# Linear attention and a mixture of experts on one core: the rarely needed blocks spread their outputs by 0/1 matmuls and SP transfers

## The chip, the cores and the metric

The kernel runs on one core of a Trainium2 chip. A core has TensorE (PE: matmuls; PEld in the profile is its weight load), VectorE (DVE), ScalarE (ACT), GpSimd (POOL), and SyncE (SP, which here only issues transfers). Each has its own instruction queue, and they wait for one another by semaphores. Transfers are made by 16 DMA engines; this kernel issues them from SP's, ACT's and Pool's queues. The metric is the device time of one execution in microseconds (us), as the median of several runs.

## The reference

The input x has 4 batches of 512 tokens with 256 features. Two layers follow, each added to its own input:

```python
x = x + attention(layernorm(x), ...)          # linear attention, 16 heads of 16
x = x + ffn(layernorm(x), gate, w0, w1, wo)   # mixture of 8 experts, the best 2 for each token
# ffn:
gate_logits = x @ gate                        # 8 per token
top_k_weights = softmax(the two largest)
out = sum over the two experts e:  weight * ((silu(x @ w0[e]) * (x @ w1[e])) @ wo[e])
```

The expert weights are 256 x 512 (w0, w1) and 512 x 256 (wo). So 2048 tokens with two experts each give 4096 rows of expert work, and how many go to which expert depends on the data.

## The kernel before, in words

**Stages.** The attention of each batch runs as a generator of 15 steps; batch b begins 4 steps after batch b - 1. Each batch writes its new x to the DRAM tile `y` (L386, on ACT's queue) and then, for each of its tokens and both chosen experts, sends a row (256 features, weight, token number) to a region of the DRAM tile `xg` that belongs to the expert: eight indirect transfers per batch on Pool's queue (L469), 32 in all.

**Blocks.** The expert work goes by blocks of 128 rows of one expert. For each block, `fetch` loads the rows from `xg` (SP's queue), `turn` transposes them and copies the expert's w0 and w1 into a staging area, `half` (L618) and `hidden` make silu(h0) * h1, and `finish` (L631 to L656) multiplies by the third weights (L640), scales each row by its weight (L645) and scatter-adds the 128 rows to their tokens by an indirect transfer on Pool's queue (L649). `advance` keeps four blocks in flight, one in each of these steps.

**How many blocks.** It isn't known when the program is built how many full blocks there are. FULL = 32 is the most there can be, USUAL = 28, SURE = 25 and EARLY = 9. Nine blocks ("early") start before the last batches are through; eight more ("last") are the part-filled ends of the experts' regions. Of the others ("full"), 16 are always there, three more usually, and those from `USUAL - EARLY` = 19 on are called `rare`: four blocks. `plan` makes a table of rows and experts; a block that doesn't exist is pointed at spare rows and does its work on those. The number of full blocks found is written to `found` (L564).

**Where results go.** The early and last blocks and the first three full ones are added to `y`. Ahead of the first block of `held` one transfer on Pool's queue copies `y` to the output (L648); the 16 held blocks are then added to the output itself (`whole`).

**The end.** At L710 every engine reads `found`, and at L711 a runtime branch (`tc.If`) asks if more than 19 full blocks were found. If so, the body runs: it zeroes `y` by four SP transfers, runs the rare blocks (which are scatter-added to `y` by four Pool transfers), loads `y` back batch by batch on SP's queue, and adds it to the output by four accumulating transfers on Pool's queue (L720 to L725). If not, every engine jumps to a skipping path[...]; its instructions carry the line L711. Behind both paths lies the program's end (L767): SP waits for all counts, each engine drains, and a barrier over the five engines closes the kernel.

Of the kernel before, what the change touches and what calls it, by code (L numbers as in the profile page):

```python
# [9 lines left out]
F32 = mybir.dt.float32  # L10
I32 = mybir.dt.int32
U32 = mybir.dt.uint32
AF = mybir.ActivationFunctionType
ALU = mybir.AluOpType
# [7 lines left out]
P = 128  # L22
# [9 lines left out]
def kernel(  # L32
# [29 lines left out]
    nc = tc.nc  # L62
    B, N, E = x.shape
    NE, _, M = w0.shape
    NT = N // P
# [6 lines left out]
    USUAL = FULL - NE // 2  # L72
    EARLY = 2 * N * TOPK // P - NE + 1
# [6 lines left out]
    xpool = ctx.enter_context(tc.tile_pool(name="x", bufs=B))  # L80
    carry = ctx.enter_context(tc.tile_pool(name="carry", bufs=2))
    work = ctx.enter_context(tc.tile_pool(name="work", bufs=2))
# [3 lines left out]
    psum = ctx.enter_context(tc.tile_pool(name="psum", bufs=8, space=PSUM))  # L86
# [18 lines left out]
    y = dram.tile([T + P, E], F32, name="y")  # L105
# [29 lines left out]
    for e in range(NE):  # L135
        for i, src in enumerate((w0, w1)):
            nc.sync.dma_start(
                out=hw_sb[i][:, bass.ts(e, OW)].rearrange("p (c m) -> p c m", c=EC),
                in_=src[e].rearrange("(c p) m -> p c m", p=P),
# [4 lines left out]
    def load_w2():  # L144
# [13 lines left out]
        out=head_mask, in_=head_mask, compare_op=ALU.is_ge, fill=0.0, base=0,  # L158
        pattern=[[-HEAD_DIM, HPC], [0, HEAD_DIM]], channel_multiplier=1,
    )  # L160
    nc.gpsimd.affine_select(
        out=head_mask, in_=head_mask, compare_op=ALU.is_ge, fill=0.0, base=HEAD_DIM - 1,
        pattern=[[HEAD_DIM, HPC], [0, HEAD_DIM]], channel_multiplier=-1,
# [6 lines left out]
        out=upto, in_=upto, compare_op=ALU.is_ge, fill=0.0, base=0,  # L170
        pattern=[[1, NE], [-1, NE]], channel_multiplier=0,
# [5 lines left out]
        out=earlier, in_=earlier, compare_op=ALU.is_ge, fill=0.0, base=-1,  # L177
        pattern=[[1, P]], channel_multiplier=-1,
# [4 lines left out]
    def counting(name, shape, pattern, base=0, per_partition=0, dtype=F32):  # L183
        t = const.tile(shape, dtype, name=name)
        nc.gpsimd.iota(
            t, pattern=pattern, base=base, channel_multiplier=per_partition,
            allow_small_or_imprecise_dtypes=True,
        )
        return t
# [8 lines left out]
    rows = counting("rows", [1, FULL], [[P, FULL]])  # L198
# [374 lines left out]
    def read(entry, most, *engines):  # L573

        loads, (value,) = nc.values_load_multi_w_load_instructions(  # L575
            entry, engines=list(engines), min_val=0, max_val=most,
            skip_runtime_bounds_check_because="plan() keeps it within them",
        )
        for ins in loads:
            tc.keep_in_program_order(ins)  # L580
        return value
# [49 lines left out]
    def finish(block, g, it):  # L631

        j, b, e, row, place = block
        if e is not None:
            at = e * OW
        else:
            at = read(place, (NE - 1) * OW, mybir.EngineType.PE)
        ps = psum.tile([P, E], F32, tag="a", name=f"eo_{j}")
        for m in range(MC):
            nc.tensor.matmul(  # L640
                ps, lhsT=it[:, m, :], rhs=w2_sb[:, bass.ds(at + m * E, E)],
                start=(m == 0), stop=(m == MC - 1),
            )
        ys = blk.tile([P, E], F32, tag="ys", name=f"ys_{j}")
        nc.vector.tensor_scalar(ys, ps, g[:, E : E + 1], None, ALU.mult)  # L645
        full = block in held
        if full and block is held[0]:
            nc.gpsimd.dma_start(out=whole, in_=y[0:T, :])  # L648
        ins = nc.gpsimd.indirect_dma_start(  # L649
            out=whole[:, :] if full else y[:, :], out_offset=bass.IndirectOffsetOnAxis(ap=g[:, E + 1 : E + 2].bitcast(I32), axis=0),  # L650
            in_=ys, in_offset=None, bounds_check=(T if full else T + P) - 1, oob_is_err=True, compute_op=ALU.add,
        )
        if full:
            return
        tc.declare_no_dep(ins.ins, group=f"after {b}", reason="tokens of batches up to b")
        tc.add_to_no_dep_group("adds", ins.ins)  # L656

    whole = out.rearrange("b n e -> (b n) e")
    fetched, turned, made, held = [], [], [], []

    def advance(block=None):


        if block is not None:
            fetched.append(fetch(block))
        if fetched and (len(fetched) > 1 or block is None):
            turned.append(turn(*fetched.pop(0)))
        block = turned.pop(0) if turned and (len(turned) > 1 or not fetched) else None
        if block:
            s = work.tile([P, MC, P], F32, tag="s", name=f"s_{block[0][0]}")  # L670
            nc.scalar.activation(s, half(0, *block), AF.Silu)
        if made:
            finish(*made.pop(0))
        if block:
            made.append(hidden(s, *block))


    state = {"staged": 0, "turned": 0, "count": spread}
# [5 lines left out]
    for at in range(max(begin) + STAGES + 1):  # L684
# [11 lines left out]
        if ready:  # L696
            block = ready.pop(0)
# [4 lines left out]
    pad(end)  # L702
    blocks = plan(tot, FULL - EARLY, B - 1, "full")
    held += blocks[: SURE - EARLY]
    rare = blocks[USUAL - EARLY :]
    for block in last + blocks[SURE - EARLY : USUAL - EARLY] + held:
        advance(block)
    while fetched or turned or made:
        advance()
    many = read(state["found"], FULL, *ENGINES)  # L710
    with tc.If(many > USUAL - EARLY):  # L711
        zero = xpool.tile([P, NT, E], F32, tag="x", name="zero")
        nc.gpsimd.memset(zero, 0.0)
        for b in range(B):
            nc.sync.dma_start(out=y[b * N : (b + 1) * N, :].rearrange("(t p) e -> p t e", p=P), in_=zero)
        for block in rare:
            advance(block)
        while fetched or turned or made:
            advance()
        for b in range(B):  # L720
            extra = xpool.tile([P, NT, E], F32, tag="x", name=f"extra_{b}")
            nc.sync.dma_start(out=extra, in_=y[b * N : (b + 1) * N, :].rearrange("(t p) e -> p t e", p=P))
            nc.gpsimd.dma_start(
                out=out[b].rearrange("(t p) e -> p t e", p=P), in_=extra, accum_op=ALU.add
            )  # L725


# [43 lines left out]
```

## Time and profile before

| what | value |
|---|---|
| median of the runs | 348.0 us (3 runs, 347.77 to 349.11) |
| the profiled execution's own time | 349.94 us |
| its span, first to last instruction | 348.1 us |
| mean granted TensorE clock in it | 0.949 |
| PE busy / PEld busy | 303.4 us (87%) / 266.6 us (77%) |
| DVE busy / ACT busy / POOL busy | 155.5 us / 127.3 us / 113.3 us |
| transfers | 35.59 MB in 27873 packets |
| of these on Pool's (software) queue | 6768 packets, 11.08 MB |

A row of the group table reads: line, engine, operation, output<-input, number of instructions | busy us in all, mean ns of one | idle time of the engine ahead of them in us, and what ended it. Register, branch, semaphore and drain instructions are not counted as busy; the profile lists them for a line under the engine's name with a q (POOLq is Pool's sequencer). For such a line it gives the durations (least, median, most) in ns and when the first and the last of them started, in us from the span's start.

### The profile page before, as it was taken

To read this page: it belongs to the slowest core of one execution; us is meant where nothing else is said; L and a number is where in the kernel's file an instruction comes from. 1 tells how busy PE (TensorE), PEld (TensorE's weight loads), DVE (VectorE), ACT (ScalarE), POOL (GpSimd) and SP (SyncE) were. 2 spreads that over 40 slices of the span, in tenths; PEclk is the share of its full clock that TensorE was granted. 3 is DMA by queue.
4 is the path that set the end of the run, shared out by engine and by line. 5 is a ranking of instruction groups with operands and counts; after the bars stand their busy time and mean duration, and the time that the engine had idled before them with its cause. 6 is when DMAs were issued, how large, how long until landed. Compare 5 with 4: busy or idle time off the path is not lost. (4 is left out here: it accounts for less than half of the span.)

```text
span 348.1 us, 6093 instructions
## 1 busy us (share of the span) xinstructions
PE 303.4 (87%) x2136; PEld 266.6 (77%) x2136; DVE 155.5 (45%) x525; ACT 127.3 (37%) x200; POOL 113.3 (33%) x147
## 2 busy tenths in 40 slices
PE   0999899899852898995999999999999999999930
PEld 0567686676741787995999999999999999999920
DVE  4856879785793662643312212232332323334110
ACT  1446738556333155352212111342433334243100
POOL 5510301347055075355322313233203333323230
PEclk9999999999975799998799999999999999999985
DMA  7999021072372632236423233332372334321220
GB/s 211 368 386 385 25 70 55 1 221 84 105 260 82 200 115 49 32 93 179 96 48 48 46 50 48 58 45 49 45 258 38 55 61 63 47 30 19 29 35 0
DMA packets 27873, 35.59 MB, mean 102 GB/s; under 512 B 2849, under 2 KB 22689, under 8 KB 27809
## 3 DMA queue, kind: packets, MB, share of 16 engines
q1 hardware_dynamic: 18960, 22.00, 19.8%
q0 software_dynamic: 6768, 11.08, 17.4%
q10 hardware_dynamic: 2112, 2.10, 2.0%
q8 instruction: 19, 0.31, 0.4%
q14 instruction: 14, 0.11, 0.1%
HBM read 22.89 MB, written 14.37 MB: 107 GB/s over the span
## 5 line engine op out<-in xcount | busy, mean ns | idle before, releaser
L618 PE MATMUL hp_full<-arena 128*128 128x128 f32 x608 | 73.9, 275 | 0.0
L618 PEld LDWEIGHTS hp_full<-arena 128*128 128x128 f32 x608 | 72.3, 192 | 1.0
L649 POOL DMA_INDIRECT out_dram<-ys_full,g_full x16 | 25.2, 1574 | 58.9 <-DVE ys_full L645 27.8
L618 PE MATMUL hp_early<-arena 128*128 128x128 f32 x288 | 37.7, 284 | 5.3 <-issue 3.6
L618 PEld LDWEIGHTS hp_early<-arena 128*128 128x128 f32 x288 | 36.2, 200 | 5.3 <-issue 3.0
L469 POOL DMA_INDIRECT xg<-hn,idx_i x32 | 32.3, 1009 | 24.2 <-issue 10.2
L640 PE MATMUL eo_full<-arena,it_full 128*128 x152 | 36.1, 380 | 0.9 <-DVE it_full L628 0.9
L618 PE MATMUL hp_last<-arena,w_sb 128*128 128x128 f32 x256 | 31.2, 275 | 0.0
L618 PEld LDWEIGHTS hp_last<-arena,w_sb 128*128 128x128 f32 x256 | 30.5, 192 | 0.4
L640 PEld LDWEIGHTS eo_full<-arena,it_full 128*128 128x128 f32 x152 | 27.4, 190 | 4.0 <-DVE it_full L628 1.0
L610 ACT COPY arena<-w_sb 128x1024 f32 x28 | 29.3, 1046 | 2.8 <-DVE mv L222 1.3
L645 DVE TENSOR_SCALAR ys_full<-eo_full,g_full 128x256 f32<-128x256 f32 x19 | 9.2, 483 | 45.0 <-PE eo_full L640 45.0
L602 ACT COPY arena<-gp_full 128x256 f32<-128x256 f32 x19 | 7.1, 372 | 59.6 <-PE gp_full L599 56.4
L628 DVE TENSOR_TENSOR it_full<-s_full,hp_full 128x512 f32<-128x512 f32 x19 | 13.1, 687 | 26.0 <-PE hp_full L618 26.0
L265 POOL TENSOR_TENSOR x<-x,bo 128x256 f32<-128x256 f32 x16 | 12.1, 782 | 37.7 <-DVE arena L248 30.3
L649 POOL DMA_INDIRECT y<-ys_early,g_early x9 | 14.0, 1557 | 28.1 <-DVE ys_early L645 24.6
L649 POOL DMA_INDIRECT y<-ys_last,g_last x8 | 12.4, 1548 | 31.8 <-DVE ys_last L645 31.8
L379 PE MATMUL ap<-wo,arena 128*128 128x256 f32 x64 | 17.5, 431 | 3.8 <-DVE arena L371 2.5
L610 DVE COPY arena<-w_sb 128x1024 f32 x28 | 19.6, 701 | 1.6 <-issue 1.4
L379 PEld LDWEIGHTS ap<-wo,arena 128*128 128x128 f32 x64 | 13.4, 217 | 7.0 <-DVE arena L371 3.2
L640 PE MATMUL eo_early<-arena,it_early 128*128 x72 | 18.3, 400 | 0.4 <-DVE it_early L628 0.4
L277 PE MATMUL qp<-arena,wqk 128*128 128x512 f32 x32 | 16.6, 667 | 0.2 <-ACT arena L270 0.2
(168 smaller groups left out, 442.6 us busy)
## 6 DMA issues: line engine op xcount, KB each, us to landing
w_sb<-in_w_dram SPq DMA_DIRECT2D x16, 512.0 KB
arena<-in_w_dram SPq DMA_DIRECT2D x8, 512.0 KB
g_full<-xg SPq DMA_DIRECT2D x19, 130.0 KB
x<-in_x_dram SPq DMA_DIRECT2D x4, 512.0 KB
y<-x ACTq DMA_DIRECT2D x4, 512.0 KB
xg<-empty SPq DMA_DIRECT2D x9, 130.0 KB
g_early<-xg SPq DMA_DIRECT2D x9, 130.0 KB
g_last<-xg SPq DMA_DIRECT2D x8, 130.0 KB
```

Source lines behind the costliest of these rows:

```text
L265: nc.gpsimd.tensor_tensor(xb[:, t, :], xb[:, t, :], bo_sb, ALU.add)
L277: nc.tensor.matmul(ps, lhsT=wqk_sb[:, k, bass.ts(c, P)], rhs=xT[:, k, :], start=(k == 0), stop=(k == EC - 1),)
L379: nc.tensor.matmul(ps[:, t - t0, :], lhsT=yT[:, c, bass.ts(t, P)], rhs=wo_sb[:, c, :], start=(c == 0), stop=(c == EC - 1),)
L469: apart(nc.gpsimd.indirect_dma_start(out=xg[:, :], out_offset=bass.IndirectOffsetOnAxis(ap=idx_i[:, t, k : k + 1], axis=0), in_=hn[:, t, k ...
L602: nc.scalar.copy(gT, ps)
L610: copy(w[i], hw_sb[i][:, bass.ds(at, OW)])
L618: nc.tensor.matmul(ps[:, m, :], lhsT=w[i][:, bass.ds(k * M + m * P, P)], rhs=gT[:, k, :], start=(k == 0), stop=(k == EC - 1),)
L628: nc.vector.tensor_tensor(it, s, ps, ALU.mult)
L640: nc.tensor.matmul(ps, lhsT=it[:, m, :], rhs=w2_sb[:, bass.ds(at + m * E, E)], start=(m == 0), stop=(m == MC - 1),)
L645: nc.vector.tensor_scalar(ys, ps, g[:, E : E + 1], None, ALU.mult)
L649: ins = nc.gpsimd.indirect_dma_start(out=whole[:, :] if full else y[:, :], out_offset=bass.IndirectOffsetOnAxis(ap=g[:, E + 1 : E + 2].bit ...
```

## The change

`finish` gets an early end for rare blocks: instead of the scatter-add, the scaled rows are kept in an SBUF tile (`made`), and their token numbers in a column of another (`whose`). In the body of the `tc.If`, `y` isn't used any more. A row of numbers 0 to 511 is made once by Pool's iota. For each batch, SP loads the output's rows; DVE compares the token numbers with the row of numbers, which gives a 0/1 matrix for each of the four rare blocks, and lowers the token numbers by 512 for the next batch; PE multiplies these matrices with the kept rows, four matmuls summed in PSUM for each of four tiles of 128 tokens; DVE adds the sums to the loaded rows, and SP stores them. The body has no transfer on Pool's queue any more. Ahead of the branch, the only difference is that `rare` is made as an empty list first and filled in place.

```diff
@@ finish
+        if block in rare:
+            k = rare.index(block)
+            nc.vector.tensor_scalar(state["made"][:, k, :], ps, g[:, E : E + 1], None, ALU.mult)
+            nc.vector.tensor_copy(state["whose"][:, k : k + 1], g[:, E + 1 : E + 2].bitcast(I32))
+            return
         ys = blk.tile([P, E], F32, tag="ys", name=f"ys_{j}")
...
-    fetched, turned, made, held = [], [], [], []
+    fetched, turned, made, held, rare = [], [], [], [], []
...
-    rare = blocks[USUAL - EARLY :]
+    rare += blocks[USUAL - EARLY :]
...
     with tc.If(many > USUAL - EARLY):
-        zero = xpool.tile([P, NT, E], F32, tag="x", name="zero")
-        nc.gpsimd.memset(zero, 0.0)
-        for b in range(B):
-            nc.sync.dma_start(out=y[b * N : (b + 1) * N, :].rearrange("(t p) e -> p t e", p=P), in_=zero)
+        state["made"] = xpool.tile([P, NT, E], F32, tag="x", name="rare_made")
+        lists = xpool.tile([P, NT, E], F32, tag="x", name="lists").rearrange("p t e -> p (t e)")
+        numbers, state["whose"] = lists[:, 0:N], lists[:, N : N + len(rare)]
+        nc.gpsimd.iota(
+            numbers, pattern=[[1, N]], base=0, channel_multiplier=0, allow_small_or_imprecise_dtypes=True
+        )
+        sums = [xpool.tile([P, NT, E], F32, tag="x", name=f"sums_{i}") for i in range(2)]
         for block in rare:
             advance(block)
         while fetched or turned or made:
             advance()
         for b in range(B):
-            extra = xpool.tile([P, NT, E], F32, tag="x", name=f"extra_{b}")
-            nc.sync.dma_start(out=extra, in_=y[b * N : (b + 1) * N, :].rearrange("(t p) e -> p t e", p=P))
-            nc.gpsimd.dma_start(
-                out=out[b].rearrange("(t p) e -> p t e", p=P), in_=extra, accum_op=ALU.add
-            )
+            rows = out[b].rearrange("(t p) e -> p t e", p=P)
+            nc.sync.dma_start(out=sums[b % 2], in_=rows)
+
+            at = []
+            for k in range(len(rare)):
+                at.append(work.tile([P, N], F32, tag="ex", name=f"at_{b}_{k}", bufs=4))
+                nc.vector.tensor_scalar(at[k], numbers, state["whose"][:, k : k + 1], None, ALU.is_equal)
+            nc.vector.tensor_scalar(state["whose"], state["whose"], -float(N), None, ALU.add)
+            for t in range(NT):
+                ps = psum.tile([P, E], F32, tag="a", name=f"spread_{b}_{t}")
+                for k in range(len(rare)):
+                    nc.tensor.matmul(
+                        ps, lhsT=at[k][:, bass.ts(t, P)], rhs=state["made"][:, k, :],
+                        start=(k == 0), stop=(k == len(rare) - 1),
+                    )
+                nc.vector.tensor_tensor(sums[b % 2][:, t, :], sums[b % 2][:, t, :], ps, ALU.add)
+            nc.sync.dma_start(out=rows, in_=sums[b % 2])
```

## The prediction

> **What bounds the kernel now.** I read the group table first, to see whether the edited block runs at all in this measurement.
>
> ```profile
> L618 PE MATMUL hp_full<-arena 128*128 128x128 f32 x608 | 73.9, 275 | 0.0
> ...
> L649 POOL DMA_INDIRECT out_dram<-ys_full,g_full x16 | 25.2, 1574 | 58.9 <-DVE ys_full L645 27.8
> ...
> L469 POOL DMA_INDIRECT xg<-hn,idx_i x32 | 32.3, 1009 | 24.2 <-issue 10.2
> ```
>
> A block costs two halves of 8 matmuls, each of which appears as two MATMULs: 32 per block. So `hp_full` x608 is 19 blocks, exactly USUAL - EARLY = 28 - 9. The four rare blocks would make it 23. The condition is false here, on every engine: all of the edited work (zeroing, spreading, adding) is skipped before and will be skipped after. A saving or a loss can come only from the branch, from what the skipping path does instead, and from the kernel's end behind it.
>
> So I looked at the end. First the chain of work that ended last, in order of time:
>
> ```profile
> 335.40 0.03 POOLq L575
> 335.43 1.27 POOL out_dram L649
> ```
>
> This chain ends at 336.7 us, but the span is 348.1 us: for 11.4 us (3.3% of the span) no engine does any counted work. The instructions of the `tc.If` line and of the end (L711 and L767) fill it; columns are duration min/median/max in ns, then first and last start in us:
>
> ```profile
> L711 POOLq EVENT_SEMAPHORE  x5: 17/43/43, 335.7 to 339.4; - x5
> L711 PEldq EVENT_SEMAPHORE  x2: 51/51/51, 337.0 to 337.1; - x2
> L711 PEldq COMPARE_BRANCH  x1: 3645/3645/3645, 333.3 to 333.3; - x1
> L711 DVEq COMPARE_BRANCH  x1: 72/72/72, 334.8 to 334.8; - x1
> L711 POOLq COMPARE_BRANCH  x1: 53/53/53, 335.5 to 335.5; - x1
> L711 POOLq INC_SWDGE_SEM  x1: 1564/1564/1564, 339.5 to 339.5; - x1
> ```
>
> ```profile
> L767 SPq EVENT_SEMAPHORE  x14: 17/28/28, 341.0 to 348.1; - x14
> L767 POOLq EVENT_SEMAPHORE  x4: 17/17/17, 346.9 to 348.0; - x4
> L767 POOLq DRAIN  x3: 113/188/5709, 341.1 to 347.7; - x3
> L767 SPq DRAIN  x3: 7/7/7, 341.8 to 347.1; - x3
> ```
>
> Read in time: Pool issues the last scatter-add (335.2 to 336.7). Its branch falls through to the skipping path, where five semaphore instructions run, the last at 339.4: they hold Pool until its transfers have landed, about 339.2 (in the table of stretches the DMA share is 0.49 from 338 to 339 us and 0.00 after). Then one INC_SWDGE_SEM takes 1.56 us (339.5 to 341.1). It is there because the skipped block holds transfers on Pool's queue[...]. Then Pool's DRAIN lasts 5.71 us (341.1 to 346.8). SP, which waits for the raised counts, is done at 341.8; everything else waits for Pool's drain. From 346.9 the closing barrier takes 1.3 us to the end. So the last 9 us belong to Pool alone: wait, INC_SWDGE_SEM, DRAIN, barrier.
>
> **The change part by part.**
>
> The body: 64 matmuls on PE, about 40 DVE instructions (16 comparisons, 4 subtractions, 16 additions, 4 copies) and one iota come in; one memset, four scatter-adds and four accumulating transfers on Pool's queue, four zeroing transfers and four loads on SP's queue go out, and four loads and four stores on SP's queue come in. None of it runs here: 0 us. It would cost time only if `found` exceeded 19.
>
> The last scatter-add before the branch stays (in `finish`, the early return is for rare blocks only), so its issue still ends at 336.7 and its landing still releases the waiters near 339.2.
>
> INC_SWDGE_SEM: with no Pool-queue transfer left in the body there is nothing for it to make up, so it and the four landing waits ahead of it go from Pool's path: from 336.7, Pool's last counted work, to 341.1, the drain's start, 4.4 us. Pool's other skip instruction (its own semaphore, at 335.7) stays for the iota.
>
> The DRAIN: here the trace does not say what its 5.71 us are. Two causes fit. (a) It goes through the software transfers issued before it: 32 (L469) + 36 (L649: 9 + 8 + 3 + 16) + 1 (L648) = 69, so 83 ns each. (b) It waits for something that INC_SWDGE_SEM left running. The nearest rows are Pool's other drains:
>
> ```profile
> L761 POOLq INC_SWDGE_SEM  x1: 31/31/31, 0.2 to 0.2; - x1
> ...
> L761 POOLq DRAIN  x1: 183/183/183, 0.4 to 0.4; - x1
> ```
>
> At the start an INC_SWDGE_SEM of 31 ns is followed by a drain of 183 ns, before any transfer; the two drains at the end take 113 and 188 ns. The long one is the first after 69 transfers and also the first after a long INC_SWDGE_SEM, so these rows exclude neither. I take (a): SP's wait for the raised counts is already over at 341.0, so INC_SWDGE_SEM has visibly done its work before the drain starts. And nothing else happens in the 5.7 us: the DMA share is 0.00 from 339 to 347 us[...]. Bounds of the drain in the new kernel: about 0.2 us (all of it was INC_SWDGE_SEM's) and 5.7 + 1.6 = 7.3 us (the two shared one walk, and the drain now does all).
>
> Sum for (a): drain from 336.7 for 5.7 us to 342.4, barrier 1.3 us, end at 343.7 instead of 348.1: 4.4 us less. The profiled execution took 349.94 us around that span of 348.1; the median of the runs shown is 348.0. The 1.8 us around the span do not change, so I take the 4.4 us off the median: 343.6 us.
>
> What is late next: SP's end waits. Now they run from 341.0 to 341.8, i.e. 0.8 us; then they start at the landing (339.2) and end near 340.0, hidden behind the drain by 2.4 us. If the drain were gone, they would be the path: 340.0 + 0.1 + 1.3 = 341.4.
>
> [...] INC_SWDGE_SEM at 1.56 us stands on the path, while SP's own skip instructions (nine of 12 to 72 ns) ran at 299 to 301 us, beside other work. [...] The body grows on DVE and PE and shrinks on Pool. PE is charged already and ends at 337.3, hidden. If DVE starts to stall and I charge it PE's 3.6 us, it is ready at 335.6 + 3.6 = 339.2: hidden behind Pool's drain (342.4), and by 0.8 us behind SP's 340.0 if that drain goes. [...]
>
> **The rivals.**
>
> The drain goes with INC_SWDGE_SEM (cause b). For it: the two stand next to each other, and the start's short pair fits too. Against it: the raised counts have been seen before the drain begins. Then SP's waits end it: 341.4, which is 6.7 us less than 348.1: 341.3 us.
>
> The drain's 5.7 us begin only when the last transfer has landed: 339.2 + 5.7 + 1.3 = 346.2, 1.9 us less: 346.1 us. For it: today the drain stands behind that landing anyhow, so the trace can't exclude it. Against it: the transfers before the last have long landed and could be gone through meanwhile.
>
> The change does not do what it says: an increment on the skipping path remains (some Pool transfer still counted in the block). Then 348.0. Against it: every Pool transfer in the diff's body is removed, and rare blocks return ahead of the scatter-add.
>
> Slower: INC_SWDGE_SEM does a part of the clearing that the drain then does not have to do. The place is Pool's drain, the price is its growth; the point is 346.8 - 336.7 = 10.1 us, 146 ns for each of 69 transfers instead of 83. Even with the whole 1.6 us added it is 7.3 us, ending at 345.3 and giving 345.2, still faster; so slower needs a walk nearly twice as long as anything shown.
>
> **How the numbers follow.** Likeliest, (a): 0.58, 343.6, with 342.7 if the drain overlaps the last issue (it could start at 335.8) and 345.2 with the walk's share added. Cause (b): 0.25, 341.3. Drain after landing: 0.08, 346.1. Nothing changes: 0.05. Slower: 0.04. The range 340.8 to 345.3 takes in (a) with its bounds and (b) less 0.5 us of run-to-run spread (the runs lie 347.77 to 349.11), and leaves 0.17 out. A measurement of this kernel can tell about 0.5% (1.7 us) from no change. Faster by more: 0.58 + 0.25 + 0.05 of the landing case (346.1 is just beyond 346.3) = 0.88; within: 0.03 + 0.05 = 0.08; slower: 0.04.
>
> **What would show it.** Right: `hp_full` still x608; no INC_SWDGE_SEM at the `tc.If` line; Pool's long drain of about 5.7 us starting near 336; SP's waits ending near 340; the span near 343.7. A drain under 0.3 us shows (b); a drain ending at 344.9 shows the landing case[...]. Wrong would be the whole argument if any engine works differently before 335 us: the code ahead of the branch is the same, and its times should agree to within 0.3 us.

## The result and the profile after

The changed kernel takes 343.2 us (median of 6 runs, 341.67 to 344.51) against 347.9 us of the kernel before (6 runs, 347.13 to 349.11): ratio 0.9856, 95% interval 0.9821 to 0.9891, or 4.7 us less. The forecast was 343.6 us, range 340.8 to 345.3.

The rare blocks still do not run, so no run here shows what the new body costs when it is needed. The group table of the changed kernel (`finish` has grown by five lines, so its scatter-add is L654 now) has the same counts:

```profile
L618 PE MATMUL hp_full<-arena 128*128 128x128 f32 x608 | 73.9, 275 | 0.0
...
L654 POOL DMA_INDIRECT out_dram<-ys_full,g_full x16 | 25.1, 1567 | 59.0 <-DVE ys_full L650 32.3 <-issue 12.2 <-DVE it_full L628 11.4
```

In order of time, Pool's last scatter-add in the changed kernel (start us, us):

```profile
334.10 1.54 POOL L654 DMA_INDIRECT out_dram<-ys_full,g_full  x1 [3.08 <-DVE ys_full L650]
```

Instructions of the `tc.If` line (now L716) and of the end (now L787):

```profile
L716 PEldq COMPARE_BRANCH  x1: 3365/3365/3365, 332.2 to 332.2; - x1
L716 DVEq COMPARE_BRANCH  x1: 72/72/72, 333.7 to 333.7; - x1
L716 POOLq COMPARE_BRANCH  x1: 53/53/53, 334.4 to 334.4; - x1
L716 POOLq EVENT_SEMAPHORE  x1: 17/17/17, 334.6 to 334.6; - x1
```

```profile
L787 SPq EVENT_SEMAPHORE  x14: 17/28/28, 339.1 to 342.7; - x14
L787 POOLq EVENT_SEMAPHORE  x4: 17/17/17, 342.0 to 342.7; - x4
L787 POOLq DRAIN  x3: 46/118/7249, 334.7 to 342.5; - x3
L787 SPq DRAIN  x3: 7/7/7, 339.8 to 342.2; - x3
```

INC_SWDGE_SEM is gone, and so are four of Pool's five semaphore instructions; in the trace of before the first of those four starts at 339.20, just behind the last landing (339.17). Pool comes to its drain at 334.7, while the last scatter-add is still being issued (334.1 to 335.6), and not at 341.1. The drain is still the long one: it ends at 334.71 + 7.25 = 341.96 (starts with two decimals are the trace's own), 6.3 us behind the end of the issue. SP's waits now run from 339.1 (the landing) to 339.8, beside it.

The two profiled spans differ by 5.3 us, which splits so: the last issue ends at 335.6 instead of 336.7 (1.1 us, ahead of the edited place); from there to the end of the drain it is 6.3 us instead of 10.1 (3.8 us); the closing barrier takes 0.8 us instead of 1.3 (0.5 us). The first part can't be put down to the change: with the code ahead of the branch unchanged, the last issue ends anywhere from 332.1 to 335.6 us in the profiles of the changed kernel and of E3 and E6 below. So what is worked out from the end alone is safer than the difference of two spans. Nor can the third part be put down to the change (see the barrier below).

### The profile page after: what moved, and what is told of

Read it like the earlier page. It is cut to its first block, busy times and chain, and to the rows that moved or that the text cites. A ratio compares the mean times of both kernels' runs of the same rounds, so it can differ in the third digit from the quotient of the medians.

```text
span 342.8 us, 6088 instructions
## 1 busy us (share of the span) xinstructions
PE 302.6 (88%) x2136; PEld 266.3 (78%) x2136; DVE 155.4 (45%) x525; ACT 127.1 (37%) x200; POOL 113.2 (33%) x147
## 5 line engine op out<-in xcount | busy, mean ns | idle before, releaser
L654 POOL DMA_INDIRECT out_dram<-ys_full,g_full x16 | 25.1, 1567 | 59.0 <-DVE ys_full L650 32.3
L265 POOL TENSOR_TENSOR x<-x,bo 128x256 f32<-128x256 f32 x16 | 12.1, 784 | 37.0 <-DVE arena L248 29.4
L654 POOL DMA_INDIRECT y<-ys_early,g_early x9 | 14.0, 1557 | 28.0 <-DVE ys_early L650 24.7
L654 POOL DMA_INDIRECT y<-ys_last,g_last x8 | 12.4, 1548 | 31.8 <-DVE ys_last L650 31.8
```

The source lines that it names most:

```text
L265: nc.gpsimd.tensor_tensor(xb[:, t, :], xb[:, t, :], bo_sb, ALU.add)
L654: ins = nc.gpsimd.indirect_dma_start(out=whole[:, :] if full else y[:, :], out_offset=bass.IndirectOffsetOnAxis(ap=g[:, E + 1 : E + 2].bit ...
```

## The experiments

The theory on trial (A): Pool's closing drain goes through every software transfer issued since the last drain (the "listed" ones), at 83 ns each, and what the change gained is that this walk no longer has to wait for the last landing and INC_SWDGE_SEM. Rivals: the drain has a fixed price (B); it runs for a fixed time past the last landing (C); the long drain is what INC_SWDGE_SEM leaves behind. E1 to E4 ran on one chip (kernel before there 347.1 us, 344.45 to 348.51), E5 to E8 on another (346.7 us, 345.54 to 348.43). The totals expected were counted from the 343.2 us above; the changed kernel took 341.6 us beside E6 to E8 (that is E5) and did not run beside E1 to E4. So the totals are the weak part of the expectations, and the readings of the end are the strong one.

**E1, 32 more transfers.**

```diff
+    tiny = dram.tile([32, 8], F32, name="tiny")
+    for i in range(32):
+        nc.gpsimd.dma_start(out=tiny[i : i + 1, :], in_=experts[0:1, :])
     running = [attention(b) for b in range(B)]
```

> The changed kernel with 32 more tiny transfers (32 bytes each, to a spare DRAM tile) on Pool's queue in the first 40 us, where Pool has room. 69 software transfers become 101. Theory A (Pool's closing drain goes through every software transfer issued since the last drain, 83 to 91 ns each): the drain grows by 2.7 to 2.9 us and, if the rest keeps its times, the kernel takes about 346.0 us instead of 343.2. Theory B (the drain's length is a fixed price of having used the queue) and theory C (the drain runs for a fixed time past the last landing): drain of 7.2 us as before, 343.2 us.

Measured: 351.6 us (350.51 to 352.36), ratio to the kernel before 1.0134 (1.0062 to 1.0206). The last scatter-add and the end's rows:

```profile
339.86 1.54 POOL L654 DMA_INDIRECT out_dram<-ys_full,g_full  x1 [3.09 <-DVE ys_full L650]
```

```profile
L790 SPq EVENT_SEMAPHORE  x14: 17/28/28, 343.5 to 350.5; - x14
...
L790 POOLq DRAIN  x3: 46/118/9251, 340.5 to 350.3; - x3
```

The drain ends 340.48 + 9.25 - 341.40 = 8.33 us behind the issue: 8.33 / 101 = 82.5 ns for each transfer, against 5.71 / 69 = 82.7 in the kernel before. B falls, and C too: the end is 6.2 us behind the landing (343.5), and was 2.9 in the changed kernel. The total missed the 346.0 of the expectation by 5.6 us, and the rest did not keep its times: Pool's additions of the bias to x (L265) came behind the new transfers, the first at 41.9 us instead of 12.5, and the expert work began at 129.5 instead of 121.3.

**E2, drains in between.**

```diff
+    DRAINS = (6, 12, 18, 24, 30, 35)
@@ finish, behind the scatter-add
+        state["done"] = state.get("done", 0) + 1
+        if state["done"] in DRAINS:
+            tc.keep_in_program_order(nc.gpsimd.drain())
```

> The changed kernel with a drain instruction on Pool's queue behind the 6th, 12th, 18th, 24th, 30th and 35th of the 36 scatter-adds. Theory A: each drain leaves little for the next; the first, with about 38 transfers before it, takes some 3.5 us, the others under 1 us past their last landing, and the closing drain, with one transfer before it, ends with that transfer's landing (about 339.1 in the profile). SP's waits are then the last: the end comes about 2 us earlier, 341.2 us. Theory B: the closing drain still takes its 6 to 7 us, 343.2 us or more. Theory C: it still ends 2.9 us past the last landing, 343.2 us.

Measured: 339.35 us (338.53 to 339.64), ratio 0.9789 (0.972 to 0.9857). The drains in between (L661):

```profile
L661 POOLq DRAIN  x6: 4167/4295/5911, 167.5 to 325.4; - x6
```

The 6th scatter-add, which the first of these drains follows:

```profile
167.75 1.87 POOL L655 DMA_INDIRECT y<-ys_early,g_early  x1 [3.35 <-DVE it_early L629]
```

The end:

```profile
L791 SPq EVENT_SEMAPHORE  x14: 17/28/28, 335.7 to 337.3; - x14
L791 POOLq EVENT_SEMAPHORE  x4: 17/17/17, 336.5 to 337.2; - x4
L791 POOLq DRAIN  x3: 46/118/4695, 331.1 to 337.1; - x3
```

The closing drain looks long again, 4.7 us. Read it by its end: 331.08 + 4.70 = 335.78, just behind the landing that releases SP at 335.7. It has one transfer listed and ends 0.1 us behind that landing. Now SP's waits come last, and the barrier starts at 336.5. The six drains in between cost nothing that shows: from the first to the last matmul of the full blocks' halves it is 104.6 us here, as in the changed kernel. Their 4.2 us and more are not a walk of six transfers either: each record begins 0.2 us ahead of the record of the scatter-add that it follows in the program. The five later ones end 2.4 to 2.5 us behind that issue, about when a scatter-add lands (2.1 to 2.5 us in the profiles of E1, E3 and E6). The first, with 38 transfers listed, ends at 173.4, 3.8 us behind the issue's end (169.6); 38 at 83 ns would be 3.2. The total came 1.9 us below the 341.2 expected.

**E3, one Pool transfer back in the skipped body.**

```diff
-            nc.sync.dma_start(out=rows, in_=sums[b % 2])
+            (nc.sync if b < B - 1 else nc.gpsimd).dma_start(out=rows, in_=sums[b % 2])
```

> The changed kernel with one of the four stores of the skipped body (the last batch's) on Pool's queue again, so that the skipping path has one INC_SWDGE_SEM, for one semaphore of the eight. That semaphore's last transfer before the branch is the second last scatter-add but some, so Pool does not wait for the last landing. Theory A with the prediction's account of the gain (4.4 us = wait for the last landing 2.8 + INC_SWDGE_SEM 1.6): the wait is not back, the instruction is, at up to 1.6 us, partly beside the last scatter-add's issue: 343.2 to 344.8 us. Rival (any INC_SWDGE_SEM on the path brings the whole price back): 347.9 us.

Measured: 341.8 us (340.6 to 341.98), ratio 0.9853 (0.9783 to 0.9923): 5.3 us less than the kernel before on this chip, so no loss of gain shows.

```profile
331.14 1.54 POOL L654 DMA_INDIRECT out_dram<-ys_full,g_full  x1 [3.08 <-DVE ys_full L650]
```

```profile
L716 POOLq INC_SWDGE_SEM  x1: 1544/1544/1544, 331.8 to 331.8; - x1
```

```profile
L787 POOLq DRAIN  x3: 46/113/5709, 333.4 to 339.6; - x3
```

INC_SWDGE_SEM is back, as long for the one Pool transfer in the body as for the eight before (1544 and 1564 ns). But it does not wait for the last landing here (which releases SP's waits at 335.1) and runs from 331.8 to 333.3, mostly beside the issue (331.1 to 332.7): only 0.6 us of it are exposed. The eight semaphores of the expectation are in the trace of before: the last eight scatter-adds raise eight different ones (111 to 118), and the last but one landed at 334.38, the last at 339.17. The instruction as such is not the price; its place behind the last landing is.

**E4, the kernel before with the six drains** (the edit of E2, made in the kernel before).

> The kernel before with the same six drains on Pool's queue behind scatter-adds. Theory A: the wait for the landing stays, INC_SWDGE_SEM stays (1.6 us, or less if it too goes through the transfers that are still listed), the closing drain shrinks from 5.7 us to about 0.2: 342.4 us, or 341.2 if INC_SWDGE_SEM shrinks to 0.4. The prediction's rival (the long drain belongs to INC_SWDGE_SEM): drain still 5.7 us, 347.9 us.

Measured: 339.7 us (339.17 to 340.9), ratio 0.9796 (0.9728 to 0.9864).

```profile
L715 POOLq EVENT_SEMAPHORE  x5: 17/43/43, 332.1 to 336.9; - x5
...
L715 POOLq INC_SWDGE_SEM  x1: 190/190/190, 337.3 to 337.3; - x1
```

```profile
L771 SPq EVENT_SEMAPHORE  x14: 17/28/28, 337.5 to 339.0; - x14
...
L771 POOLq DRAIN  x3: 46/112/131, 337.6 to 338.8; - x3
```

The eight transfers in the skipped body, the wait for the landing and INC_SWDGE_SEM are all there, and yet the long drain is 131 ns. So it never belonged to INC_SWDGE_SEM, which is the prediction's first rival. INC_SWDGE_SEM itself falls from 1564 to 190 ns when 1 transfer is listed and not 69: it seems to go through the list too, by an estimate from these two figures at (1564 - 190) / 68 = 20 ns each. E2 and E4 on one chip (339.35 and 339.7, overlapping runs) say what the change is worth once the list is short: nothing that can be measured. E4's total is 7.4 us below the kernel before on this chip and below both numbers expected. The end explains 5.4 us of it (from the last issue's end to the kernel's end it is 6.1 us, and was 11.4); where the other 2 us come from is not shown.

**E5, the changed kernel again**, beside E6 to E8.

> The changed kernel itself, beside the next three on one chip. Expected by every theory: about 4.7 us less than the kernel before, the closing drain about 6.3 us past the end of the last scatter-add's issue.

Measured: 341.6 us (340.48 to 343.0), ratio 0.9863 (0.9818 to 0.9908).

```profile
330.58 1.54 POOL L654 DMA_INDIRECT out_dram<-ys_full,g_full  x1 [3.09 <-DVE ys_full L650]
```

```profile
L787 SPq EVENT_SEMAPHORE  x14: 17/28/28, 335.0 to 338.6; - x14
...
L787 POOLq DRAIN  x3: 46/118/6647, 331.2 to 338.4; - x3
```

The drain ends at 331.19 + 6.65 = 337.84, 5.7 us behind the issue (332.1) and not the 6.3 expected: 69 transfers at 83 ns. The landing (335.0) is 2.8 us behind the issue; it was 3.5 in the first profile after.

**E6, Pool waits for the last landing.** `ys` of the last block is kept in `state["last_ys"]`, which the memset writes; it waited for that scatter-add's transfer (2.35 us in the second row of the profile below).

```diff
+    nc.gpsimd.memset(state["last_ys"][:, 0:1], 0.0)
     many = read(state["found"], FULL, *ENGINES)
```

> The changed kernel with one memset on Pool ahead of the branch, into the last block's output tile, so that Pool waits for the last scatter-add to land before it comes to the branch and its drain; no INC_SWDGE_SEM. Theory A in its new form (the wait for the landing is what the kernel before paid, because the drain's walk of the listed transfers can't start before it): the drain starts 2.5 to 3.4 us later, the memset and the branch's load add up to 0.9 us: 3 to 4 us more than the changed kernel, 346.0 to 347.2 us. Rival (the price was INC_SWDGE_SEM itself, 1.6 us and what it leaves to the drain): 343.2 us, or the drain shorter by what it no longer has to wait for.

Measured: 343.8 us (342.23 to 344.9), ratio 0.991 (0.9881 to 0.9939): 2.2 us more than E5.

```profile
331.56 1.54 POOL L654 DMA_INDIRECT out_dram<-ys_full,g_full  x1 [3.09 <-DVE ys_full L650]
335.46 0.10 POOL L716 MEMSET ys_full<- 128x1 f32 x1 [2.35 <-DMA out_dram<-ys_full,g_full]
```

```profile
L789 SPq EVENT_SEMAPHORE  x14: 17/28/50, 335.4 to 342.8; - x14
...
L789 POOLq DRAIN  x3: 46/113/5709, 336.3 to 342.6; - x3
```

In the profile the drain starts 336.3 - 333.1 = 3.2 us behind the issue and lasts 5709 ns, to the nanosecond what it was in the kernel before and in E3. There is no INC_SWDGE_SEM here. From the last matmul to the end it is 12.1 us, against 8.9 in E5: 3.2 us, within the 3 to 4 expected. The medians show 2.2, which is less than expected (runs of each kernel lie 2.5 to 2.7 us apart), and 343.8 is below the 346.0 expected; so it is the profile that speaks for the theory here.

**E7, two drains in between** (E2 with `DRAINS = (18, 34)`).

> The changed kernel with drains on Pool's queue behind the 18th and the 34th scatter-add only. Theory A: they take about 5 us (some 50 transfers) and 2 to 4.5 us, the closing drain ends with the last landing as with six drains: 339.4 us, 4 us less than the changed kernel. If drains work only when little has gathered, the closing drain stays long: 341 us or more.

Measured: 338.8 us (337.79 to 339.95), ratio 0.978 (0.9733 to 0.9827): 2.8 us less than E5 on the same chip, the best version found.

```profile
L661 POOLq DRAIN  x2: 4717/5408/6100, 232.2 to 320.5; - x2
```

The scatter-adds that they follow:

```profile
232.45 1.54 POOL L655 DMA_INDIRECT y<-ys_full,g_full  x1 [3.96 <-DVE ys_full L651]
```

```profile
320.74 1.54 POOL L655 DMA_INDIRECT out_dram<-ys_full,g_full  x1 [3.98 <-DVE ys_full L651]
```

The end:

```profile
L791 SPq EVENT_SEMAPHORE  x14: 17/28/28, 334.4 to 336.0; - x14
...
L791 POOLq DRAIN  x3: 46/118/3267, 331.3 to 335.8; - x3
```

The two drains end 4.3 and 2.9 us behind the issues that they follow, with 50 and 17 transfers listed. The closing drain, with two listed, ends at 331.28 + 3.27 = 334.55, with the landing (334.4). The median gain over E5 is 2.8 us and not the 4 expected: what is late next is the landing and then SP's waits of 0.8 us.

**E8, no branch.** Left out: the reading of `found`, the `tc.If` and the four rarely needed blocks, which do not run on this data.

> The changed kernel without the reading of the number found, the branch and the rarely needed blocks behind it (left out: those four blocks; they are not run on this data anyway). Theory A: the branches lie beside the last scatter-add and Pool's drain, which keeps its 6.3 us past the issue: 343.2 us, at most 0.5 less. Rival (the jump over the bigger body, PE's 3.4 us, is a part of the end): 340 us or less.

Measured: 342.3 us (340.44 to 343.13), ratio 0.9852 (0.9801 to 0.9902), against 341.6 for E5 with overlapping runs.

```profile
333.00 1.54 POOL L654 DMA_INDIRECT out_dram<-ys_full,g_full  x1 [3.08 <-DVE ys_full L650]
```

```profile
L756 POOLq DRAIN  x3: 46/113/7492, 332.8 to 340.8; - x3
```

The drain ends at 332.77 + 7.49 = 340.26, again 5.7 us behind the issue (334.5), and from the last matmul to the end it is 8.9 us in both. So PE's branch (3345 ns in E5, absent here) and the bigger body are not a part of the end.

## Why the prediction was right

**That nothing but the end could change** held in the main: the counts are the same, and the profiles differ at the `tc.If` line and behind it, apart from the spread that unchanged code shows. That spread was set far too small: the prediction wanted the times ahead of the end to agree to within 0.3 us, and the last issue ends 1.1 us earlier in the profile after, and up to 4.6 us earlier in those of E3, E5 and E6, on other chips. So that 343.2 us lies 0.4 us from the forecast is in part luck; the runs of the changed kernel alone lie 2.8 us apart.

**INC_SWDGE_SEM and the wait ahead of it, 4.4 us.** Held, most exactly in E5: from the end of the last issue to the end of the drain it is 5.7 us, against 10.1 before: 4.4 us. In the first profile after it was 3.8, since the drain took 6.3 us from there, 0.6 us more (see the next point). The split of the 4.4 needs a correction that the prediction did not make: of the two terms (2.8 us waiting, 1.6 us instruction) the wait is the cause. E3 has the instruction without the wait and loses 0.6 us at most; E6 has the wait without the instruction and pays 3.2 us in its profile. The 1.6 us counted only because they, too, stood behind the landing.

**The drain as a walk of 69 transfers at 83 ns.** That the drain's length follows the number of listed transfers is shown: 82.7 ns each in the kernel before and in E6, 83 in E5, 82.5 with 101 transfers (E1), and 131 ns for the drain behind six drains, the last landing and INC_SWDGE_SEM (E4). What the drain does in that time no profile shows: the walk is the author's picture of these lengths. The upper bound of 7.3 us, by which the drain would take over INC_SWDGE_SEM's share, is not needed: 5709 ns with that instruction ahead (before, E3) and without it (E6). The 7249 ns of the profile after are a record that begins 0.9 us ahead of the issue's end.

The plain walk leaves some ends unexplained: 6.3 us for 69 transfers in the profile after, 3.8 for 38 (E2), 4.3 for 50 and 2.9 for 17 (E7). One reading, the author's estimate from these ends, fits them all: half of the walk comes behind the last landing, whenever that is. In the profile after the landing was late (339.1, 3.5 us behind the issue), and the drain ended 341.96 - 339.10 = 2.86 us behind it, half of 5.71. Where the landing came within 2.86 us of the issue (E3, E5) it cost nothing. For the drains in between, half of 83 ns for each transfer behind a landing at 2.3 us (E6) gives, as an estimate, 3.9, 4.4 and 3.0 us, each within 0.1 of what was measured; the plain walk, or the landing where that comes later, gives 3.2, 4.2 and 2.3. No run was made to test this reading.

**What is late next.** SP's waits ending near 340 were found at 339.8, hidden. That they become the path once the drain is gone was seen in E2 and E7.

**The branches.** DVE's and Pool's take 72 and 53 ns as before, though the body has grown on DVE; PE's takes 3.4 us (3.6 before, 3.3 to 3.9 in E1 to E6), hidden, as E8 shows. Why PE's is the long one was not shown.

**The barrier** was taken over at 1.3 us and is 0.8 in the changed kernel. In the profiles of E1 to E8 it takes 0.8 to 0.9 us too (counted from SP's last wait in E2, E4 and E7, where that comes last; E4's end is the code of the kernel before). The 1.3 us occur in the one profile of before alone. The excess is on Pool: 0.36 us in which it stands still ahead of its last drain (0.03 in the profile after), and 188 ns for that drain in place of 46. E4 has a gap of the same length in another place, between its last semaphore instruction (336.9) and INC_SWDGE_SEM (337.3); what Pool waits for in them is not settled.

**The landing rival.** The rival with the drain starting only at the landing (346.1 us) falls by the profile after itself, where the drain ends 2.9 us behind the landing and not 5.7; by the reading above, half of it was right.

## What to carry to other kernels

Where the page's chain of work ends long before the span does, list the semaphore, branch and drain instructions behind it: they are not counted as busy, and 11.4 us lay there. A body that does not run can still cost time on its skipping path: here, eight transfers on Pool's queue inside a rarely run body put a wait for the last landing (2.8 us) and an INC_SWDGE_SEM (1.6 us) ahead of everything that followed on Pool. This kernel paid for all of its 69 transfers on Pool's queue in the closing drain (5.7 us); drains behind earlier scatter-adds took that over here, and from the first to the last matmul of the full blocks' halves it stayed 104.6 us (E2). Six such drains alone took the kernel before from 347.1 to 339.7 us (E4; 5.4 us of it at the end), more than the change did (347.9 to 343.2), and two took another 2.8 us off the changed kernel (338.8 against 341.6, E7).

## What was not expected of the hardware

Pool's closing drain took 82.5 to 82.9 ns for each software transfer since the last drain, in kernels with 69 and 101 of them, although all but the last had landed before (in the kernel before the last but one at 334.4, 6.7 us ahead of the drain; in the one profile with a late landing it took 0.6 us more); with 32 transfers of 32 bytes among them (E1) the mean was 82.5 ns, and 82.7 with none. INC_SWDGE_SEM took 1544 ns for one skipped transfer and 1564 ns for eight with 69 transfers listed, and 190 ns for eight with one listed, after drains: in these three profiles its length went with the number listed and not with what was skipped.
